# Two graph-attention layers in fp32: the query matrix by halves, the last rows at once, exponentials in even portions

## Chip, cores, metric

One core of a Trainium2 chip. The metric is the device time of one execution in microseconds (us), as the median of several executions; lower is better. Every run quoted gave a correct result. A ratio is the mean time of one kernel's fast runs over the mean of the fast runs of the kernel before in the same rounds, so it is not quite the quotient of the medians that are quoted beside it. A number in brackets after it is the 95% interval.

## The reference

```python
# N = 2708 rows, D = 1024, fp32; adj about 1% ones
h = relu(layernorm(x))                              # layer 0
e = relu((h @ Wf + bf) @ (h @ Wg + bg).T)
x = x + softmax(where(adj > 0, e, -9e15), axis=1) @ (h @ W + bW)
h = relu(layernorm(x))                              # layer 1
hW = h @ W1;  f1, f2 = hW @ a1, hW @ a2
e = leaky_relu(f1 + f2.T, 0.2)
x = x + relu(softmax(where(adj > 0, e, -9e15), axis=1) @ hW)
```

All biases are zero in the data.

## The kernel before

Layer 0 is not computed as written. The kernel forms M = Wf Wg^T once, then q = h M, scores = q h^T plus rank-one terms for the biases, and it projects by W only after the aggregation. The rows fall into five **panels** of queries (586, 586, 512, 512, 512) and eleven **pairs** of row tiles; pair 2 is the **short pair**, two tiles of 74 rows. Each large product is done with seven half-size products M1 to M7 in place of eight (the scheme of Strassen and Winograd), so operands are first added and subtracted on VectorE and stored to device memory (`hs_d` for the scores, `hg_d` for the aggregation, `md_d` for q), then loaded as needed.

Work off TensorE's path is handed out by credit. Each group of matmuls may draw a number of microseconds of background work:

```python
def put(us, go, fetch=None, takes_psum=False):
    later.append([us, fetch, go, takes_psum])

def behind(us, psum_free=False):            # called after a group of matmuls
    credit[0] = min(credit[0] + us, 2 * us)
    while later and credit[0] > 0 and (psum_free or not later[0][3]):
        credit[0] -= one()                  # the first item of `later`, whole
```

An item is drawn whole as soon as any credit is left. The order of instructions on each engine is fixed when the program is built.

A pair is normalized in place (`norms`), its sums for the aggregation are stored (`rows`), its dot products taken (`dots`), it is transposed, and its sums for the scores are stored (`sums`):

```python
EARLY = 6
for q in range(NQ):                         # NQ = 11
    put(4.2, norms(q), fetch(q));  put(2.7, rows(q));  put(3.2, dots(q))
    if q < EARLY:
        put(0.5, transposes(q), takes_psum=True);  put(2.7, last(q))   # last: sums, stores
for q in range(EARLY, NQ):
    put(0.5, transposes(q), takes_psum=True);  put(2.7, last(q))
# ... sums(q): the short pair's stores are cut to n = 74 of 128 columns (296-byte runs)
    nc.gpsimd.dma_start(hs_d[q][:, 0:4, :, :n]..., lo[:, :, :, :n]...)
```

The end of a projection in layer 0 adds the residual and stores it; then the rows of layer 1 are made:

```python
def go(t, e, c):                            # e: left or right half of the row tile t
    add(xs[t][e], c, xs[t][e])
    nc.gpsimd.dma_start(x1_d[t][:n, ...], xs[t][e])
    if seen[t] == 2:
        rows_done(t, xs[t])                 # put(2.1, normalize); put(3.2, dots); ...
```

In layer 1 an item of the exponentials is one row tile of P, handed out at 2.0 while a projection group gave a credit of 6.0.

## Time and profile before

| | before |
|---|---|
| median of three runs | 3357.59 us (3354.02 to 3358.53) |
| span of the profiled execution | 3363.8 us |
| TensorE busy | 94% |
| sum of TensorE's gaps over 0.5 us | 185 us |

TensorE is the bound, so what counts is its gaps and the slow matmuls that follow them (16 passes took 8.53 us after a gap of 10.00, and 7.03 before it). "L414" in a line is line 414 of the kernel; the figure in square brackets is the idle time of the engine before the group and what ended it. The lines that carry this are in the prediction below.

### The profile page before, as it was taken

The page shows a single profiled execution, that of the slowest core. Times are in us where ns is not written, and L with a number is a line of the kernel's source. Part 1 is how long each engine was busy: PE and PEld are TensorE (multiplying, and loading weights), DVE is VectorE, ACT ScalarE, POOL GpSimd, SP SyncE. Part 2 cuts the span into 40 slices and gives each one's busy share as a digit, 9 for nine tenths or more (in the row PEclk, how much of TensorE's full clock was granted, in tenths as well). Part 3 has the DMA queues.
Part 4 walks back from the last instruction along what each step waited for, and adds up shares of the span by engine and source line. Part 5 has one row for each costly group of instructions (what it writes and reads, how often), then busy time and mean ns, then how long its engine had stood idle before and what let it go on. Part 6 is the DMA issues. An engine that isn't in the chain of part 4 may idle for free.

```text
span 3363.8 us, 34967 instructions
## 1 busy us (share of the span) xinstructions
PE 3165.5 (94%) x12924; PEld 2336.2 (69%) x12924; DVE 1733.8 (52%) x3606; ACT 497.5 (15%) x832; POOL 369.9 (11%) x423
## 2 busy tenths in 40 slices
PE   8768999999999989999999999996989999999998
PEld 4346776757877468885888885854757738678584
DVE  5666568165541664616672358449273362734612
ACT  2222020010110100201020002004040120301200
POOL 1421001210002110011000102020010000000001
PEclk9889999999999989999999999997999999999999
DMA  5898658576643576547664466675435355454645
GB/s 206 264 335 278 210 183 313 177 219 194 196 147 132 166 208 215 178 157 236 205 210 158 143 215 214 235 258 198 144 124 201 127 166 189 150 203 153 209 140 197
DMA packets 273714, 660.56 MB, mean 196 GB/s; under 512 B 54604, under 2 KB 124224, under 8 KB 272264
## 3 DMA queue, kind: packets, MB, share of 16 engines
q1 hardware_dynamic: 237080, 543.04, 49.3%
q0 software_dynamic: 36464, 115.29, 9.9%
q8 instruction: 102, 1.67, 0.2%
q14 instruction: 68, 0.56, 0.0%
HBM read 542.97 MB, written 115.13 MB: 196 GB/s over the span
## 4 chain that ended last, share of the span: by engine, by line
PE 40%; issue 6%; DVE 4%; DMA 1%; POOL 1%; ACT 0%; SPq 0%; POOLq 0%; DVEq 0%; ACTq 0%
PE gz L414 10%; PE gy L414 8%; PE gx L414 8%; PE sz L833 3%; PE pz L731 3%; PE sx L833 2%; PE sy L833 2%; PE py L731 1%; DVE P L1014 1%; DVE sm L198 1%; DVE P L198 1%; PE px L731 1%; PE qz L414 1%; PE qy L414 0%; PE qx L414 0%
## 5 line engine op out<-in xcount | busy, mean ns | idle before, releaser
L833 PE MATMUL sz<-B,As 128*128 128x256 f32 (+3 forms) x1320 | 334.0, 396 | 14.7 <-DVE st L198 14.0
L414 PE MATMUL gz<-P,hc 128*128 128x256 f32 (+3 forms) x1320 | 307.6, 392 | 0.0
L833 PEld LDWEIGHTS sz<-B,As 128*128 128x128 f32 (+1 forms) x1320 | 246.4, 188 | 77.3 <-DVE st L198 19.5
L414 PEld LDWEIGHTS gz<-P,hc 128*128 128x128 f32 (+1 forms) x1320 | 248.6, 190 | 48.7
L833 PE MATMUL sx<-B,As 128*128 128x256 f32 (+3 forms) x880 | 229.4, 403 | 15.1 <-DMA As<-hs_d 13.0
L414 PE MATMUL gx<-P,hc 128*128 128x256 f32 (+3 forms) x880 | 211.7, 401 | 11.8 <-ACT P L1016 11.8
L833 PE MATMUL sy<-B,As 128*128 128x256 f32 (+3 forms) x880 | 219.3, 391 | 0.7 <-DMA As<-hs_d 0.7
L414 PE MATMUL gy<-T,hc 128*128 128x256 f32 (+3 forms) x880 | 206.2, 395 | 6.4 <-DMA hc<-hg_d 6.4
L668 POOL TENSOR_TENSOR gT<-gT,rr 128x2048 f32<-128x2048 f32 (+3 forms) x20 | 68.3, 3437 | 1307.3 <-ACT rr L137 742.6
L414 PEld LDWEIGHTS gx<-P,hc 128*128 128x128 f32 (+1 forms) x880 | 169.6, 194 | 54.0 <-ACT P L1016 18.8
L414 PE MATMUL gz<-Sa,hc 128*128 128x256 f32 (+3 forms) x880 | 206.7, 393 | 0.0
L731 PE MATMUL py<-w,ps 128*128 128x512 f32 (+1 forms) x352 | 168.0, 630 | 37.2 <-DVE pt L198 30.7
L833 PEld LDWEIGHTS sx<-B,As 128*128 128x128 f32 (+1 forms) x880 | 163.1, 191 | 51.9 <-DMA As<-hs_d 14.1
L414 PEld LDWEIGHTS gy<-T,hc 128*128 128x128 f32 (+1 forms) x880 | 168.1, 191 | 43.0 <-DMA hc<-hg_d 7.8
L833 PEld LDWEIGHTS sy<-B,As 128*128 128x128 f32 (+1 forms) x880 | 162.9, 185 | 39.0 <-DMA As<-hs_d 1.1
L414 PEld LDWEIGHTS gz<-Sa,hc 128*128 128x128 f32 (+1 forms) x880 | 165.4, 190 | 32.1
L198 DVE TENSOR_TENSOR gT<-gz,m 128x256 f32<-128x256 f32 (+1 forms) x80 | 34.7, 438 | 269.5 <-PE gz L414 269.5
L731 PEld LDWEIGHTS py<-w,ps 128*128 128x128 f32 (+1 forms) x352 | 68.9, 198 | 130.6 <-issue 93.4
L731 PE MATMUL pz<-w,ps 128*128 128x512 f32 (+1 forms) x352 | 155.5, 593 | 0.4 <-DMA w<-wt_d 0.3
L731 PE MATMUL px<-w,gT 128*128 128x512 f32 x320 | 142.2, 595 | 5.4 <-ACT P L1013 3.0
L537 ACT COPY mask<-mk_ps 128x1024 bf16<-128x1024 bf16 (+1 forms) x55 | 55.6, 1010 | 611.2 <-PE mk_ps L536 336.6
L731 PEld LDWEIGHTS pz<-w,ps 128*128 128x128 f32 (+1 forms) x352 | 65.3, 186 | 86.8 <-issue 83.7
(237 smaller groups left out, 4609.0 us busy)
## 6 DMA issues: line engine op xcount, KB each, us to landing
hc<-hg_d SPq DMA_DIRECT2D x280, 704.0 KB
As<-hs_d SPq DMA_DIRECT2D x150, 512.0 KB
w<-wt_d SPq DMA_DIRECT2D x96, 512.0 KB
w<-in_L_gnn_W_dram SPq DMA_DIRECT2D x72, 512.0 KB
md<-md_d SPq DMA_DIRECT2D x70, 512.0 KB
adj_i<-in_adj_dram SPq DMA_DIRECT2D x50, 512.0 KB
hg_d<-g POOLq DMA_DIRECT2D x40, 512.0 KB, 6.1
As<-hs_d SPq DMA_DIRECT2D x50, 256.0 KB
```

Of the source, the lines that this page charges most:

```text
L198: nc.vector.tensor_tensor(o, a, b, OP.add)
L414: nc.tensor.matmul(acc[d][:, :h], ls(k), right(m, k), start=(start and k == 0), stop=(k == K - 1), skip_group_check=True)
L537: nc.scalar.copy(mk[:n, :, :k4 * P], ps[:n, :, :k4 * P])
L668: nc.gpsimd.tensor_tensor(of(e, s), of(e, s), by(s, k), OP.mult)
L731: nc.tensor.matmul(ps, left[i][m][:, k, :], w_[k], start=(start and k == 0), stop=(k == NH - 1), skip_group_check=True)
L833: nc.tensor.matmul(ps[:n, :h], A[i // 2][:, i % 2, c, :n], B[m][c // 2][:, c % 2, :h], start=(start and c == 0), stop=(c == NH - 1), skip_ ...
L1014: nc.vector.scalar_tensor_tensor(s, ub[:n, :w], f[1][:n, t:t + 1], s, op0=OP.add, op1=OP.max)
```

## The change

Its intent: (1) make M in two column halves, so that the first product can begin with half of the right factor, and do four pairs ahead of q in place of six, with the starts of further pairs interleaved with their ends; (2) treat the last panel's rows at once as their projection ends, so that layer 1 can begin sooner; (3) hand out the exponentials of layer 1 evenly; (4) take the residual rows of the last projection from another buffer pool, so that they hold up no weights.

```diff
-    EARLY = 6
+    EARLY, AHEAD = 4, 5
...
+        for q in range(EARLY):
+            start(q)                        # norms, rows, dots
+            end(q)                          # transposes, sums and stores
+        for q in range(EARLY, EARLY + AHEAD):
+            start(q)
         for q in range(EARLY, NQ):
-            put(0.5, lambda q=q: transposes(q), takes_psum=True)
-            put(2.7, lambda q=q: last(q))
+            end(q)
+            if q + AHEAD < NQ:
+                start(q + AHEAD)
...
+    transposed_wg(0)
+    for a in range(NC):
+        half_row_of_M(a, 0)                 # first half of the columns, all eight row blocks
+        if a == NH: ... transposed_wg(1)
+        if a >= NH: behind(6.5, True)
+    for k in range(NH):
+        for a in (k, k + NH):
+            half_row_of_M(a, 1)
+            behind(6.5, True)
+        left_of_q(k)
...                                         # q's products: M1 M5 M2 M6 M3 M7 M4 before
+        accumulate(left, right, NH, h, (M1, M2, M5, M6, M3, M7, M4), then, evict, "q",
...                                         # the aggregation's second operand: after M5, not M1
-                   {M1: second, M2: fourth, ...
+                   {M5: second, M2: fourth, ...
...                                         # rows_done
+        if panel_of[t] == NP - 1:
+            normalize(xt)
+            dots()
+            raise_max(0, q, k, first_mask[t][:n, :width[0]])
+            if whole:
+                ... pair_h(1, q, ...)       # last pair: between the transposes and the reductions of shifts1(0)
+                for p in range(1, NP):
+                    put_max(p, q)
+            return
...                                         # weights1, finish1, end of the program
-            put(2.0, lambda i=i, mk=mk: go(i, mk), ...
+            front.append([2.1, ..., (lambda i=i, mk=mk: go(i, mk)), False])
+        later[:0] = front
...
-                xs[t] = row_halves("x1_res", n, True)
+                xs[t] = row_halves("x1_res", n, p < NP - 1)
...
-        project(1, p, g, finish1(), by_pair=(p == NP - 1), rate=6.0)
+        project(1, p, g, finish1(p), by_pair=(p == NP - 1), rate=1.7)
```

More of the change, by code (lines that the diff above doesn't have):

```diff
@@ L302, in last, with start, end @@
             made[0] = q + 1
-        for q in range(NQ):
-            put(4.2, lambda q=q: norms(q), lambda q=q: fetch(q))
-            put(2.7, lambda q=q: rows(q))
-            put(3.2, lambda q=q: dots(q))
-            if q < EARLY:
-                put(0.5, lambda q=q: transposes(q), takes_psum=True)
-                put(2.7, lambda q=q: last(q))
+        def start(q):
+            put(4.2, lambda: norms(q), lambda: fetch(q))
+            put(2.7, lambda: rows(q))
+            put(3.2, lambda: dots(q))
+        def end(q):
+            put(0.5, lambda: transposes(q), takes_psum=True)
+            put(2.7, lambda: last(q))
+        for q in range(EARLY):
[3 more added lines that the diff above has]
+            start(q)
         for q in range(EARLY, NQ):
-            put(0.5, lambda q=q: transposes(q), takes_psum=True)
-            put(2.7, lambda q=q: last(q))
+            end(q)
+            if q + AHEAD < NQ:
+                start(q + AHEAD)
     def make_until(q):
@@ L323, in load_rows, with transposed_wg @@
         return t
-    bfb = row_to_all(bf, "bfb")
-    wgT = [[slot(f"wgT{c}_{b}") for b in range(2)] for c in range(NC)]
-    for b in range(2):
+    bfb, bgb = row_to_all(bf, "bfb"), row_to_all(bg, "bgb")
+    wgT, wfT, M = [None, None], {}, {}
+    def transposed_wg(b):
         ws = [load_rows(wg, 4 * b + i, "wg") for i in range(4)]
+        wgT[b] = [slot(f"wgT{c}_{b}")[:, :W] for c in range(NC)]
         for c in range(NC):
@@ L332 @@
                 nc.tensor.transpose(ps[:, i * P:(i + 1) * P], ws[i][:, c * P:(c + 1) * P], ident)
-            copy(wgT[c][b][:, :W], ps)
+            copy(wgT[b][c], ps)
         for i in range(4):
             dot(u[:, 4 * b + i:4 * b + i + 1], halves(ws[i]), halves(bfb))
-    bgb = row_to_all(bg, "bgb")
-    wfT = {}
     def transposed_wf(a):
@@ L347, in transposed_wf, with store_M, half_row_of_M, left_of_q @@
         dot(v[:, a:a + 1], halves(wt), halves(bgb))
-    M = {}
-    def row_of_M(a, background):
-        M[a] = []
-        for b in range(2):
-            ps = bank("M_ps")
-            for c in range(NC):
-                nc.tensor.matmul(ps, wfT[a][c // NH][:, c % NH, :], wgT[c][b][:, :W], start=(c == 0), stop=(c == NC - 1))
-            M[a].append(slot(f"M{a}_{b}"))
-            copy(M[a][b][:, :W], ps)
-            if background:
-                behind(6.5, True)
-        wfT.pop(a)
-    def left_of_q(a):
-        k = a % NH
-        store = lambda m, s: nc.gpsimd.dma_start(md_d[:, m, k, :], s)
-        if a < NH:
-            store(M1, M[k][0][:, :W])
-            return
-        a11, a21, a12, a22 = (t[:, :W] for t in M.pop(k) + M.pop(k + NH))
+    def store_M(m, k, s):
+        nc.gpsimd.dma_start(md_d[:, m, k, :], s)
+    def half_row_of_M(a, b):
+        ps = bank("M_ps")
+        for c in range(NC):
+            nc.tensor.matmul(ps, wfT[a][c // NH][:, c % NH, :], wgT[b][c], start=(c == 0), stop=(c == NC - 1))
+        M[a, b] = slot(f"M{a}_{b}")[:, :W]
+        copy(M[a, b], ps)
+        if b == 0:
+            store_M(M1 if a < NH else M2, a % NH, M[a, b])
+    def left_of_q(k):
+        a11, a12, a21, a22 = M.pop((k, 0)), M.pop((k + NH, 0)), M.pop((k, 1)), M.pop((k + NH, 1))
         s1, s2, s4 = (slot(f"ms{i}")[:, :W] for i in range(3))
         add(s1, a21, a22)
-        store(M5, s1)
-        store(M2, a12)
+        store_M(M5, k, s1)
         sub(s2, s1, a11)
-        store(M6, s2)
+        store_M(M6, k, s2)
+        sub(s4, a12, s2)
+        store_M(M3, k, s4)
         sub(a21, a11, a21)
-        sub(s4, a12, s2)
-        store(M3, s4)
-        store(M7, a21)
-        store(M4, a22)
+        store_M(M7, k, a21)
+        store_M(M4, k, a22)
     make_pairs()
-    for i, a in enumerate((0, 4, 1, 5, 2, 6, 3, 7)):
-        if i == 0:
-            transposed_wf(0)
-            transposed_wf(4)
+    transposed_wg(0)
+    ahead = [0, 1, 2, 3, 4, 5, 6, 7]
+    for a in range(NC):
+        for _ in range(2):
+            if ahead:
+                transposed_wf(ahead.pop(0))
+        half_row_of_M(a, 0)
+        if a == NH:
             dot(c0, halves(bfb), halves(bgb))
-        if i == 2:
-            for k in (1, 5, 2, 6, 3, 7):
-                transposed_wf(k)
             vb = [slot(f"vb{g}") for g in range(2)]
@@ L394, with accumulate @@
                 spread(vb[g][:, :W], [v[:, 4 * g + j:4 * g + j + 1] for j in range(4)])
-        row_of_M(a, i >= 2)
-        left_of_q(a)
-    def accumulate(left, right, rows, K, h, then, evict, name, prepare={}, psum_after=(), rate=0.0):
-        X = None
-        for m, start in ((M1, True), (M5, True), (M2, False), (M6, True), (M3, False), (M7, False), (M4, False)):
+            transposed_wg(1)
+        if a >= NH:
+            behind(6.5, True)
+    for k in range(NH):
+        for a in (k, k + NH):
+            half_row_of_M(a, 1)
+            wfT.pop(a)
+            behind(6.5, True)
+        left_of_q(k)
+    def accumulate(left, right, K, h, order, then, evict, name, prepare={}, rate=0.0):
+        for m in order:
+            start = m in (M1, M5, M6)
             if m == M1:
@@ L487, in project_q @@
                  M4: lambda d, ps: plus(part(B[M2], d), ps, ub(d + NH), part(m1, d))}
-        accumulate(left, right, NH, NH, h, then, evict, "q",
+        accumulate(left, right, NH, h, (M1, M2, M5, M6, M3, M7, M4), then, evict, "q",
                    {M1: second, M2: fourth, M3: lambda: sides(M3), M7: lambda: sides(M7), M4: lambda: sides(M4)},
@@ L564, in load_mask, with column_max @@
         return mt
-    def column_max(p, acc):
+    def column_max(p, acc, between=None):
         m = stats.tile([P, 5], FP, name="mcol")
         nc.vector.memset(m, 0.0)
-        o = 0
+        o, turned = 0, []
         for i, (_, n) in enumerate(panels[p]):
@@ L575, in column_max @@
             nc.tensor.transpose(ps[:n, i % 4, :], acc[:, o:o + n], ident)
-            nc.vector.tensor_reduce(m[:n, i:i + 1], ps[:n, i % 4, :], AX.X, OP.max)
+            turned.append(ps[:n, i % 4, :])
             o += n
+        if between:
+            between()
+        for i, (_, n) in enumerate(panels[p]):
+            nc.vector.tensor_reduce(m[:n, i:i + 1], turned[i], AX.X, OP.max)
         return m
@@ L668, in scale @@
                 nc.gpsimd.tensor_tensor(of(e, s), of(e, s), by(s, k), OP.mult)
-        accumulate(left, right, NH, NQ, h, then, evict, "g",
-                   {M1: second, M2: fourth, M3: lambda: inverse.append(column_sum_inverse(p, sm)), M7: scale}, rate=rate)
+        accumulate(left, right, NQ, h, (M1, M5, M2, M6, M3, M7, M4), then, evict, "g",
+                   {M5: second, M2: fourth, M3: lambda: inverse.append(column_sum_inverse(p, sm)), M7: scale}, rate=rate)
         nc.vector.tensor_tensor(of(1, lo), of(1, lo), by(lo, h), OP.mult)
@@ L722, in project @@
             acc, tmp = {}, {}
-            for m, start in ((M1, True), (M2, False), (M5, True), (M6, True), (M3, False), (M7, False), (M4, False)):
+            for m in (M1, M2, M5, M6, M3, M7, M4):
+                start = m in (M1, M5, M6)
                 w_ = ws.pop(m) if m in ws else load_W(l, m)
@@ L893, in softmax, with shifts1 @@
         return sm
-    done_rows = {}
+    def shifts1(p, between=None):
+        k, t0 = len(panels[p]), first[p]
+        top = column_max(p, mx[p], between)[:, :k]
+        f1 = f[0][:, t0:t0 + k]
+        z, m, c = (stats.tile([P, 5], FP, name=nm)[:, :k] for nm in ("z", "m1", "none"))
+        nc.vector.tensor_add(z, f1, top)
+        nc.vector.scalar_tensor_tensor(m, z, ALPHA, z, op0=OP.mult, op1=OP.max)
+        nc.vector.tensor_scalar(c, top, -BIG / 2, None, op0=OP.is_ge)
+        nc.vector.tensor_mul(m, m, c)
+        nc.vector.tensor_scalar(c, top, -BIG / 2, -BIG, op0=OP.is_lt, op1=OP.mult)
+        nc.vector.tensor_add(m, m, c)
+        sub(z, f1, m)
+        nc.vector.scalar_tensor_tensor(m, f1, ALPHA, m, op0=OP.mult, op1=OP.subtract)
+        return z, m
+    done_rows, first_mask = {}, {}
     def rows_done(t, xt):
@@ L905, in dots, with met @@
             nc.vector.tensor_scalar(f2s[:n, t:t + 1], f[1][:n, t:t + 1], ALPHA, None, op0=OP.mult)
+        q, k = pair_of[t]
+        whole = all(s in done_rows for s in pairs[q])
+        if panel_of[t] == NP - 1:
[3 more added lines that the diff above has]
+            if whole:
+                if q == NQ - 1:
+                    got["zm"] = shifts1(0, lambda: pair_h(1, q, *(done_rows[s] for s in pairs[q])))
+                else:
+                    pair_h(1, q, *(done_rows[s] for s in pairs[q]))
+                for p in range(1, NP):
+                    put_max(p, q)
+            return
+        def met():
+            known.add(q)
+            for p in range(NP):
+                if generated[p] > q:
+                    put_max(p, q)
         put(2.1, lambda: normalize(xt))
         put(3.2, dots)
-        q, _ = pair_of[t]
-        if all(s in done_rows for s in pairs[q]):
-            def met():
-                known.add(q)
-                for p in range(NP):
-                    if generated[p] > q:
-                        put_max(p, q)
+        if whole:
             put(2.7, lambda: pair_h(1, q, *(done_rows[s] for s in pairs[q])))
@@ L927, in start @@
                 r0, n = tiles[t]
+                if p == NP - 1:
+                    first_mask[t] = load_mask(0, *pair_of[t])
                 xs[t] = row_halves("x_res", n, t in short)
@@ L976 @@
                                                  M7: lambda p=p: first_masks(p + 1, 2)})
+    flush()
     project(0, NP - 1, G.pop(NP - 1), finish0(NP - 1), by_pair=True)
-    flush()
-    def shifts1(p):
-        k, t0 = len(panels[p]), first[p]
-        top = column_max(p, mx[p])[:, :k]
-        f1 = f[0][:, t0:t0 + k]
-        z, m, c = (stats.tile([P, 5], FP, name=nm)[:, :k] for nm in ("z", "m1", "none"))
-        nc.vector.tensor_add(z, f1, top)
-        nc.vector.scalar_tensor_tensor(m, z, ALPHA, z, op0=OP.mult, op1=OP.max)
-        nc.vector.tensor_scalar(c, top, -BIG / 2, None, op0=OP.is_ge)
-        nc.vector.tensor_mul(m, m, c)
-        nc.vector.tensor_scalar(c, top, -BIG / 2, -BIG, op0=OP.is_lt, op1=OP.mult)
-        nc.vector.tensor_add(m, m, c)
-        sub(z, f1, m)
-        nc.vector.scalar_tensor_tensor(m, f1, ALPHA, m, op0=OP.mult, op1=OP.subtract)
-        return z, m
     def weights1(p, z, m):
@@ L1020, in go, with finish1 @@
             exps[0] += 1
+        front = []
         for i in range(len(order) + LAG):
             mk = []
-            put(2.0, lambda i=i, mk=mk: go(i, mk),
-                (lambda i=i, mk=mk: mk.append(load_mask(p, *order[i]))) if i < len(order) else None)
+            front.append([2.1, (lambda i=i, mk=mk: mk.append(load_mask(p, *order[i]))) if i < len(order) else None,
+                          (lambda i=i, mk=mk: go(i, mk)), False])
+        later[:0] = front
         return S, sm
-    def finish1():
+    def finish1(p):
         xs = {}
@@ L1046, in take_shifts @@
     def take_shifts(p):
+        flush()
         got["zm"] = shifts1(p)
@@ L1050, in take_weights @@
         got["P"] = weights1(p, *got["zm"])
-    take_shifts(0)
     take_weights(0)
```

## The prediction

> **What bounds the kernel now.** I read the page first (busy shares), then the waits, then TensorE's own timeline for the whole span, and last the busy time of each engine in chosen stretches.
>
> ```profile
> PE 3165.5 (94%) x12924; PEld 2336.2 (69%) x12924; DVE 1733.8 (52%) x3606; ACT 497.5 (15%) x832; POOL 369.9 (11%) x423
> ```
>
> TensorE is the bound: 94% of the span. So the change can only earn what TensorE now loses: its gaps, and the slow matmuls after a gap. Adding up every gap over 0.5 us in TensorE's timeline gives 185 us. They sit in four places: the start (65 us before the scores of panel 0), the scores of panels 2 and 3 (28 us), the end of layer 0 with the first exponentials of layer 1 (about 38 us) and the projections of layer 1 (40 us). The diff goes at the first, third and fourth.
>
> The start, by stretch (columns: stretch, length, busy time and count of PE, PE weight loads, DVE, ACT, POOL, then granted clock, DMA share, GB/s):
>
> ```profile
> 60.00:70.00 10.00, 10.00 (x51) 6.41 (x50) 5.25 (x9) 4.37 (x7) 1.62 (x3) 1.00 0.41 150
> ...
> 130.00:140.00 10.00, 10.00 (x24) 4.37 (x23) 0.00 (x0) 0.00 (x0) 3.14 (x4) 1.00 0.83 183
> 140.00:150.00 10.00, 0.60 (x2) 0.00 (x0) 0.55 (x1) 2.15 (x4) 2.29 (x4) 0.70 0.71 233
> ...
> 180.00:190.00 10.00, 0.00 (x0) 0.00 (x0) 9.21 (x24) 3.13 (x6) 4.32 (x9) 0.58 0.99 354
> 190.00:200.00 10.00, 0.00 (x0) 0.00 (x0) 1.48 (x5) 0.28 (x1) 1.36 (x2) 0.50 1.02 298
> ```
>
> Two idle stretches of TensorE, each with a falling clock. TensorE's timeline names what ended the second:
>
> ```profile
> 204.99 10.06 PE L414 MATMUL qx<-hT,md 128*128 128x293 f32 x32 [25.96 <-DMA md<-md_d]
> ```
>
> The product M (16 half rows at 6.95 us) ends at 179, but q's first matmul waits until 205. The load queue issues the hT tiles only at 187.6: hT shares its buffer with hsT, so it waits for the last of the six early pairs to be written out. The wait of 18.2 us at 140.6 is for x of the fifth pair, behind a VectorE that stood still from 124.3 to 149.5.
>
> A projection of layer 1 (panel 0), TensorE:
>
> ```profile
> 2473.87 7.03 PE L731 MATMUL px<-w,gT 128*128 128x512 f32 x16
> 2482.62 7.11 PE L731 MATMUL px<-w,gT 128*128 128x512 f32 x16 [1.72 <-ACT pt L737]
> ...
> 2513.46 8.53 PE L731 MATMUL py<-w,ps 128*128 128x512 f32 x16 [10.00 <-DVE pt L198]
> ```
>
> and engine busy time for it, and for the end of layer 0:
>
> ```profile
> 2216.00:2302.00 86.00, 54.66 (x127) 23.92 (x125) 63.87 (x141) 13.68 (x21) 18.74 (x22) 0.82 0.87 301
> ...
> 2474.00:2536.00 62.00, 50.28 (x115) 21.93 (x114) 49.40 (x74) 23.08 (x36) 3.86 (x7) 0.92 0.54 175
> ```
>
> In the projection VectorE is full for the first 39 us, with exponentials handed out three at a time, and part idle for the last 20: TensorE waits for an addition queued behind them.
>
> [...] clock 0.50 to 0.58 in the idle stretches above, and the 16 passes after the 10 us gap take 8.53 us, not 7.03. So a removed long gap is worth about 1.5 us more than its length. [...] the trace has 0.69 us for 128x512, so VectorE's work can simply be counted. [...] The trace has the short pair (rows of 296 B) landing in about 22 us where a full pair takes 6.5, and 298 to 354 GB/s at most over the saturated stretches. [...]
>
> **Part 1: M by halves, four pairs ahead.** (a) First M product: 28.9 us now, after all 4 MB of the right factor. Then 2 MB of it, one row block of the left and the two bias rows (about 3.5 MB at 330 GB/s, after a start of 7 us) give some 20. But the second half's transposes (4.5 us of TensorE) come later, in the middle, so by the point where the background work starts TensorE is only some 5 us ahead. (b) Four whole pairs instead of six: the last early pair is the fourth, so hT comes free some 25 to 30 us before M is done and not after it. Two pairs' transposes (3.7 us each) leave this stretch, and with no fifth pair's transposes queued before M's next half rows the wait of 18.2 us goes. VectorE will still stand some 20 us behind the short pair's write, but TensorE then has the half rows left and banks for them. (c) q's order M1, M2, M5 lets two products run on the two operands stored first.
> M then ends near 155 to 160; hT is loaded by about 165 to 172 with a busy DMA. Before, two of q's seven products were done at 225.5; after: 168+16 = 184, though M5 needs a VectorE operand, due near 180 to 190. That is a gain of about 40. The five products left take 8 us each, as now: 224 to 230. I allow 7 to 10 for loads that come late from a busy DMA, so the scores start at 231 to 240 instead of 272, **36 us** earlier. Check by bytes: 51 MB were moved by 205; two pairs' hs tiles and half a pair's rows less make 47.6. At 60 us about 13 are done; the other 34.6 at 290 GB/s take 119, so 179. q's operands are not last in line, so 168 to 175 is still possible, but DMA is now the floor.
> (d) Given back: seven pairs end inside the scores of panel 0 instead of five (+7.4 us of TensorE, but that is what left M's stretch and is counted there), and two starts. As per query pair needs 1.84 MB, masks 0.9, an end 2.1: up to 340 GB/s for the first nine query pairs, at the limit. In return the burst of four pairs' transposes at 286 (waits 4.8 and 0.7) is gone. I take 7.4 more TensorE time, 6 less waiting, and 5 of DMA waits: 6 back. **Net 30 us** (18 to 42).
>
> **Part 2: last rows of layer 0.** From TensorE's last projection matmul (2275.0) to the spread of the shifts (2295.4) are 20.4 us. After: two additions 1.8, statistics and their ACT step 2.9, dots 3.3, one maximum 0.8, transposes hidden under the pair's sums 2.7, five reductions 1.2, eight small operations 1.3: 14 us. Gained: 6. The reductions no longer alternate with the transposes, and eight of the 0.74 us maxima move behind the aggregation. Within the projection (59.3 us for 48.1 of passes) the treatment at once puts the first group's rows ahead of the second group's sums on VectorE; the wait of 5.95 may shrink or move. I take 3. **9 us** (2 to 14). The slow first product (about 14 us lost, 2.1 us an exponential, VectorE-bound) stays.
>
> **Part 3: exponentials of layer 1.** A product of two groups is 16 passes, 6.87 us; seven make 48.1 (21 groups of panel 1: 72.1). Measured from first matmul to the aggregation's first: 61.7, 81.2, 60.4, 59.7. Lost: 13.6, 9.1, 12.3, 11.6 = 46.6. After, at 1.7 us of credit and 2.1 an item, 11 exponentials fall into the 14 steps (10 having gone into the last aggregation product); the last three go behind the next aggregation, which may take them because its second step now comes after M5, not M1. VectorE then has 11 x 2.13 + 17.8 of sums and additions + 1.4 = 42.6 us in 48: tight but even. The wait for ACT's first copy (1.4 to 1.7) stays, and I allow one more per projection: 10 in all. **36 us** (28 to 41).
>
> **Part 4: the last projection.** Its residual rows move from the stream buffers to slots, so the weights' load is not held up: the wait of 6.02 on w at 3325, and the slow matmuls after it (about 1.5). **7 us.**
>
> Sum: 30 + 9 + 36 + 7 = 82; 3357.6 - 82 = **3276 us**.
>
> **Rivals.** (R1) DMA takes over at the start: the two idle stretches shrink but the waits reappear as As or md loads in q and the scores of panel 0. For: DMA share 0.94 to 1.02 from 180 to 272. Against: 0.59 to 0.61 from 360 to 420, so there is room to move into. Part 1 would then be worth 12 and the time 3294. (R2) VectorE becomes the projection's bound: 42.6 of 48 us leaves little for an order fixed in advance; half of part 3 stays lost: 3294. (R3) Treating the rows at once starves the second group: its sums wait for two tiles' norms and dots (about 13 us of TensorE), and part 2 is worth -3: 3288. (R4) Better than thought: M5 not held, no DMA waits: part 1 gives 45, time 3260.
>
> **Range and chances.** Parts 3 and 4 are the surest, part 1 the widest. Spreads of 10, 5, 5 and 2 us, and some for reordering elsewhere, give about 20: range 3250 to 3306. The 2% line is 3357.6 x 0.98 = 3290.4, some 14 us above the centre: faster 0.75, within 2% 0.24, slower 0.01.
>
> **What would show it.** First M matmul near 20; q's first matmul at 165 to 175 and the first score near 235; scores of panel 0 still about 178 long; about 14 us from the last projection matmul of layer 0 to the spread; projections of layer 1 at 50 to 52 us with no wait over 3 us on pt; no wait on w in the last. I am wrong if waits of several us on As or hT turn up in the first 400 us, or if pt waits stay.

## The result, and the profile after

| | before | after |
|---|---|---|
| median | 3358.06 us (3354.02 to 3361.71, 4 runs) | 3341.61 us (3336.16 to 3345.40, 4 runs) |
| ratio | | 0.995 [0.9932, 0.9968] |
| profiled span, granted clock | 3363.8 us, 0.971 | 3343.4 us, 0.973 |
| TensorE: first M matmul | 28.9 | 24.9 |
| last M matmul ends | 177.3 | 152.6 |
| first q matmul | 205.0 | 191.0 |
| first score | 272.0 | 254.4 |
| scores of panel 0 end | 449.9 | 452.4 |
| first projection of layer 0 starts | 672.0 | 680.8 |
| last projection of layer 0 | 2215.7 to 2275.0 | 2224.5 to 2296.2 |
| first aggregation matmul of layer 1 | 2302.4 | 2324.4 |
| last matmul | 3355.2 | 3334.8 |

The kernel is half a per cent faster, not the 2.4% predicted. The marks say where: layer 1 takes 1010.4 us in place of 1052.8, a gain of 42.4, and 22.0 of it had been lost by its beginning. The start, which was to gain 30, loses 8.8 by the first projection. From there to the last projection of layer 0 nothing changes (1543.7 us in both). That projection and the passage to layer 1 take 99.9 us in place of 86.7, a loss of 13.2.

**The start.** TensorE's timeline of the kernel after:

```profile
24.89 7.03 PE L364 MATMUL M_ps<-wgT,wfT 128*128 128x512 f32 x16
...
144.75 7.89 PE L364 MATMUL M_ps<-wgT,wfT 128*128 128x512 f32 x18
190.96 4.45 PE L422 MATMUL qx<-hT,md 128*128 128x293 f32 x9 [38.31 <-DMA md<-md_d]
...
284.94 4.28 PE L846 MATMUL sz<-B,As 128*128 128x293 f32 x8 [8.29 <-DVE st L198]
```

M is done 25 us earlier, and then TensorE waits 38 us, not 26, for q's operands. And the scores of panel 0 have two new waits of over 8 us (the other stands at 304.1), both for an addition on VectorE. DMA in two stretches of the kernel after (columns as in the prediction; the last two are DMA share and GB/s):

```profile
110.00:140.00 30.00, 29.96 (x82) 14.02 (x81) 13.47 (x35) 5.20 (x11) 11.70 (x13) 1.00 0.63 137
...
180.00:190.00 10.00, 0.00 (x0) 0.00 (x0) 0.74 (x2) 0.00 (x0) 1.04 (x2) 0.50 0.99 327
```

From 110 to 140 the DMA engines move 137 GB/s at 0.63 of their time; afterwards they are full until q can begin (350 GB/s at 1.02 from 140 to 191). ScalarE's timeline and then VectorE's show what stood still meanwhile:

```profile
141.48 0.58 ACT L272 COPY hsT<-h_ps 128x512 f32<-128x512 f32 x1 [16.55 <-DMA hs_d<-hsT]
```

```profile
127.69 0.21 DVE L176 SCALAR_TENSOR_TENSOR r<-part,c 128x1 f32<-128x1 f32 x1
144.38 0.69 DVE L201 TENSOR_TENSOR hsT<-hsT,a 128x512 f32<-128x512 f32 x1 [16.48 <-ACT a L272]
```

The fourth pair cannot be copied into hsT, which has one buffer, until the short pair has been stored out of it. VectorE waits for ScalarE, and what the two would have made is not stored. This pause is not the whole of the hole: GpSimd goes on issuing what is ready, and the rate is lowest before the pause (79 GB/s from 110 to 120, 213 from 130 to 140, inside it). The load queue waits too, 12.0 us from 107 to 119, for a store of rows (`hg_d<-x`). And q's left operands hT are loaded into the buffer that hsT leaves, so their first load is issued only 5.4 us after M's end. The load queue (SyncE) in the kernel after:

```profile
158.07 2.22 SPq L98 DMA_DIRECT2D hT<-hs_d  x2
```

The DMA issues of the kernel after, from 100 to 160 us (transfer, queue, count, KB each, us to landing), show the short pair (592 KB) against a whole pair (1024 KB), then the same for sums of the aggregation:

```profile
hs_d<-hsT POOLq DMA_DIRECT2D x2, 1024.0 KB, 10.1
...
hg_d<-g POOLq DMA_DIRECT2D x2, 512.0 KB, 8.5
hg_d<-g POOLq DMA_DIRECT2D x2, 296.0 KB, 21.0
hs_d<-hsT POOLq DMA_DIRECT2D x1, 592.0 KB, 21.7
```

**The scores of panel 0.** VectorE's timeline ahead of the wait at 276.6:

```profile
273.54 0.69 DVE L212 BATCH_NORM_STATS2 bn<-x 128x6 f32<-128x512 f32 x1
...
283.36 0.21 DVE L176 SCALAR_TENSOR_TENSOR r<-part,c 128x1 f32<-128x1 f32 x1
283.49 0.82 DVE L198 TENSOR_TENSOR sm<-sx,rb 128x293 f32<-128x293 f32 x2
```

A whole start of a pair (10 us, 273.5 to 283.4), behind the end of another (from 271.6), stands ahead of the addition `sm` that frees TensorE's banks.

**The end of layer 0.** TensorE's timeline of the kernel after (before: waits of 5.95 and 2.00 us in the projection, and 13.70 ahead of the transposes `mx_ps`):

```profile
2262.27 5.95 PE L744 MATMUL px<-w,gT 128*128 128x512 f32 x8 [9.06 <-issue]
2275.04 6.41 PE L744 MATMUL py<-w,ps 128*128 128x512 f32 x8 [6.81 <-DVE ps L198]
...
2313.32 1.33 PE L583 MATMUL mx_ps<-ident,mx 128*128 128x128 f32 x5 [17.09 <-DVE mx L807]
```

The first ends with ScalarE's copy at 2261.61. ScalarE's timeline:

```profile
2250.70 0.81 ACT L220 ACTIVATE x_res<-x_res,rs 128x512 f32<-128x512 f32 x1 [4.66 <-DMA x_d<-x_res]
...
2260.19 1.52 ACT L220 ACTIVATE x_res<-x_res,rs 128x512 f32<-128x512 f32 x2 [1.96 <-DMA x_d<-x_res]
2261.61 0.56 ACT L750 COPY pt<-px 128x512 f32<-128x512 f32 x1
```

The rows are normalized in place, in the tile that has just been handed to a store, so each activation waits until that store has read it, and the copy that TensorE needs stands behind in ScalarE's order. In the second wait VectorE shows one maximum of 6 us beside nine others of 0.70 to 0.82. VectorE, then GpSimd at the same time:

```profile
2267.03 6.03 DVE L807 SCALAR_TENSOR_TENSOR mx<-maskl,f,mx 128x586 f32<-128x586 bf16 x1
```

```profile
2267.51 4.91 POOL L976 TENSOR_TENSOR x_res<-x_res,bwb 128x512 f32<-128x512 f32 x4
```

**Layer 1.** The projection of panel 0, to compare with the lines in the prediction:

```profile
2496.66 7.03 PE L744 MATMUL px<-w,gT 128*128 128x512 f32 x16
2505.42 7.11 PE L744 MATMUL px<-w,gT 128*128 128x512 f32 x16 [1.72 <-ACT P L1042]
...
2526.09 7.03 PE L744 MATMUL py<-w,ps 128*128 128x512 f32 x16
...
2547.73 12.51 PE L422 MATMUL gx<-P,hc 128*128 128x293 f32 x50
```

The wait of 10 us is gone: 51.1 us from the first matmul to the aggregation's first, in place of 61.7. The last projection, before and then after:

```profile
3331.11 3.75 PE L731 MATMUL py<-w,ps 128*128 128x512 f32 x4 [6.02 <-DMA w<-wt_d]
```

```profile
3312.88 3.67 PE L744 MATMUL px<-w,gT 128*128 128x512 f32 x8 [0.72 <-issue]
```

No wait for w is left there (the projection of panel 1 has three new ones, 2.8 us together). Parts 3 and 4 do what was predicted; parts 1 and 2 are the question.

### The profile page after: what moved, and what is told of

The parts are those of the page before. It is cut to its first block, busy times and chain, and to the rows that moved or that the text cites. A ratio compares the mean times of both kernels' runs of the same rounds, so it can differ in the third digit from the quotient of the medians.

```text
span 3343.4 us, 34899 instructions
## 1 busy us (share of the span) xinstructions
PE 3159.0 (94%) x12924; PEld 2337.7 (70%) x12924; DVE 1743.4 (52%) x3606; ACT 498.9 (15%) x832; POOL 369.0 (11%) x423
## 4 chain that ended last, share of the span: by engine, by line
PE 43%; issue 4%; DVE 3%; DMA 1%; ACT 0%; POOL 0%; POOLq 0%; DVEq 0%; SPq 0%; ACTq 0%
PE gz L422 12%; PE gy L422 8%; PE gx L422 8%; PE sz L846 3%; PE pz L744 3%; PE sx L846 2%; PE sy L846 2%; PE px L744 2%; PE py L744 1%; DVE sm L198 1%; PE qz L422 1%; DMA w<-wt_d 0%; DVE P L1043 0%; PE qx L422 0%; PE qy L422 0%
## 5 line engine op out<-in xcount | busy, mean ns | idle before, releaser
L422 PEld LDWEIGHTS gy<-T,hc 128*128 128x128 f32 (+1 forms) x880 | 168.4, 191 | 40.2 <-DVE Sa L201 4.8
L744 PE MATMUL py<-w,ps 128*128 128x512 f32 (+1 forms) x352 | 158.7, 602 | 9.4 <-DVE ps L198 6.8
```

The costliest lines, as they stand in the source:

```text
L422: nc.tensor.matmul(acc[d][:, :h], ls(k), right(m, k), start=(start and k == 0), stop=(k == K - 1), skip_group_check=True)
L744: nc.tensor.matmul(ps, left[i][m][:, k, :], w_[k], start=(start and k == 0), stop=(k == NH - 1), skip_group_check=True)
```

## The experiments

All kernels had three rounds beside the kernel before, whose medians were 3361.59 (e1 to e4), 3362.96 (e5 to e8), 3360.91 (e9 to e12) and 3363.78 us (e13 to e15).

### e1: the change without part 1

```diff
-    EARLY, AHEAD = 4, 5
+    EARLY = 6        # and M, the order of pairs and q's order as in the kernel before
```

> The changed kernel with its first part undone: M in whole rows, six pairs ahead, q's products in the old order; the rest stays. Theory: the first part wins 17.6 us up to the first scores (254.4 against 272.0) and gives them back, 20 us in the scores of panel 0 (198 against 178) and some 6 us in the first aggregation, so it is worth about -9 us; then this kernel takes 3332 us, ratio to the kernel before 0.9925. Rival (the prediction's): the first part is a gain that something else hides; then this kernel is slower than the changed one, 3350 us or more.

Measured: 3334.38 us, 0.9921 [0.9905, 0.9938]; the first score at 272.4. Without part 1 the change is faster than with it, by 0.0029 or about 10 us. The two ran in different rounds and their intervals just touch, so the profiles have to carry it, and they agree: the first projection of layer 0 starts at 670.9 in e1 and at 680.8 with the change.

### e2: the change without part 2

```diff
-        if panel_of[t] == NP - 1:
-            normalize(xt) ... return        # all rows put behind, as before
-    flush()
     project(0, NP - 1, G.pop(NP - 1), finish0(NP - 1), by_pair=True)
+    flush()
...
+    take_shifts(0)
```

> The changed kernel with the treatment of the last rows of layer 0 undone. Theory: the treatment at once lengthens the last projection of layer 0 from 59 to 72 us and does not shorten what follows it (28.2 us against 27.4 to the first aggregation of layer 1), so undoing it gives 13 us: 3328 us, ratio 0.991. Rival: that projection is longer for another reason (what the first part left behind, or the queue of loads); then still 3341 us.

Measured: 3326.03 us, 0.9901 [0.9884, 0.9918]. Part 2 costs about 16 us. From the last projection's first matmul to the first of layer 1 it is 85.9 us here, against 99.9 with the change.

### e4: the kernel before with parts 3 and 4 alone

```diff
         # in the kernel before
-            put(2.0, ... go(i, mk) ...)
+            front.append([2.1, ..., go(i, mk), False])      # and later[:0] = front
-        project(1, p, g, finish1(), by_pair=(p == NP - 1), rate=6.0)
+        project(1, p, g, finish1(p), by_pair=(p == NP - 1), rate=1.7)
```

> The kernel before with only the exponentials of layer 1 handed out evenly, the second step of the aggregations after M5, and the last residual rows in slots. Theory: the parts add up, and this one is worth 42 us by the profiles (layer 1 from its first aggregation matmul to its last projection matmul: 1052.8 before, 1010.4 after): 3316 us, ratio 0.9875. Rival: part of the 42 us was lent by the other parts; then 3325 us or more.

Measured: 3320.92 us, 0.9882 [0.9867, 0.9896], 40 us. The two parts need nothing of the rest. With e1 and e2 the sum closes roughly: a gain of 40, less 10 and 16, leaves 14, where the change itself gives 17 (0.995).

### e3: part 2 with the normalized rows in tiles of their own

```diff
-            normalize(xt)
+            x1, xt = xt, row_halves("h1", n)
+            done_rows[t] = xt
+            normalize(x1, xt)
```

> The changed kernel, but the last panel's rows are normalized into tiles of their own and not in place: same instructions. Theory: the in-place activation has to wait until the store of the same tile has been read (4.7, 2.0, 2.3 and 4.1 us on ScalarE), which also keeps ScalarE from copying the next group's first product, so TensorE waits 9.05 us. With tiles of their own the 9.05 us go and 4 us of the tail after the last matmul: 3328 to 3332 us. Rival: the wait is VectorE's, for a mask whose load stands behind a weight load (6.8 us on TensorE); then at most 1 or 2 us change.

Measured: 3333.71 us, 0.9919 [0.9904, 0.9933]. TensorE's timeline of the last projection:

```profile
2248.59 5.33 PE L746 MATMUL px<-w,gT 128*128 128x512 f32 x8 [2.77 <-issue]
2264.08 6.13 PE L746 MATMUL py<-w,ps 128*128 128x512 f32 x8 [10.15 <-DVE ps L198]
```

The first wait falls from 9.06 to 2.77 us, so it was the store of the same tile. The second grows from 6.81 to 10.15: VectorE does its eight maxima before the sums all the same. From the projection's first matmul to the first of layer 1 it is 92.3 us (99.9 with the change, 86.7 before).

### e5: and the maxima of the other panels after the last pair

```diff
         # e3, and
-                for p in range(1, NP):
-                    put_max(p, q)
+                if q == NQ - 1:
+                    for q in range(NQ - 2, NQ):
+                        for p in range(1, NP):
+                            put_max(p, q)
```

> As e3 (last rows normalized into tiles of their own), and the maxima of panels 1 to 4 over the last two pairs are put behind only after the very last pair. Theory: with the stores out of the way, what still delays the second group's sums are eight maxima ahead of them on VectorE, which took 10.8 us in e3 because one waits for a mask whose load stands behind a weight load; TensorE waited 10.15 us. Without them there the last projection of layer 0 falls from 68 to about 58 us: 3323 us, ratio 0.989 (e3 had 0.9919). Rival: VectorE simply has too much to do in that stretch, whatever the order; then the wait moves and the ratio stays at 0.991 or more.

Measured: 3329.25 us, 0.9892 [0.9867, 0.9916], 86.9 us for the passage. The wait ahead of py is 5.39. It did not go with the maxima: the operation that now stood at that place, the first of the pair sums, took 5.95 us itself. I had put the maximum of 6 us down to a mask loaded late; a pair sum reads no mask. That was taken up in e13.

### e6: the short pair as a whole pair, padded with zeros on GpSimd

```diff
+                full = row_halves("x", P)
+                    nc.gpsimd.memset(full[e], 0.0)          # for the short tiles
-                    load(xs[q][-1][e], x[r0:r0 + n, ...])
+                    load(full[e][:n], x[r0:r0 + n, ...])
...
-            n = rows_of[q]                  # in transposes, sums and pair_h of layer 0
+            n = P
```

> The changed kernel with the short pair (74 rows each) padded by rows of zeros to 128, so that its h, sums and transposes are stored like those of a full pair and not in runs of 296 bytes from 74 rows. Theory: q's first product waits at 153 to 191 because DMA loses some 30 us of its rate between 110 and 140 (79 to 213 GB/s) behind that pair's stores; then DMA is full to 210. With whole stores (about 1.6 MB more to move, 5 us) the first q product comes 12 to 20 us earlier, near 175, and the scores near 238: about 3328 us, ratio 0.991. Rival: DMA is bound by its bytes alone from 80 on; then q starts at 191 or later and the time is 3341 us or more.

Measured: 3345.30 us, 0.9943 [0.9918, 0.9967]. A flawed test. The load queue of the kernel e6 waited for the memset:

```profile
SPq L98 <- POOL x L255: 51.4, 2, 50.9
```

M ended at 168.4 in place of 152.6, and q began at 191.2. It tells nothing of the short pair; e9 repeats it without the memset.

### e7: seven starts ahead

```diff
-    EARLY, AHEAD = 4, 5
+    EARLY, AHEAD = 4, 7
```

> The changed kernel with all seven other pairs started before the first of them is ended (seven ahead, not five), so that no norms and dots are left for the scores of panel 0. Theory: the two waits of 8.3 and 8.6 us there come from a start of 10 us and an end standing together on VectorE ahead of the next query pair's additions; without starts there the scores of panel 0 take about 180 us, not 198. The starts go into q's products, where DMA is full (2.85 MB each), so q gets longer by 4 to 12 us: 3327 to 3335 us, ratio 0.991. Rival: it is DMA that makes those scores long; then they stay near 195 us.

Measured: 3338.76 us, 0.9923 [0.9899, 0.9948]. The scores of panel 0 take 184.4 us in place of 198.0, and the waits of 8.29 and 8.63 us are gone: they were the starts in the middle of the scores. Part of it returns, for the ends now come four at once (a wait of 3.91 in the middle of their transposes), and q waits 4.41 for a right operand.

### e8: halves, but six pairs ahead

```diff
-    EARLY, AHEAD = 4, 5
+    EARLY, AHEAD = 6, 5
```

> The changed kernel with M by halves but six pairs ended ahead of q, as in the kernel before (and five started after). It splits the first part: the order of M alone. Theory: making M by halves is worth only its earlier start (some 8 us), the wait of 18 us for the fifth pair's rows comes back, q starts near 198 and the scores of panel 0 take 178 us again; so 3325 to 3335 us, ratio 0.991. Rival: the fewer pairs are what gains at the start and the halves do nothing; then q starts at 205 and the time is near that of e1, 3334 us.

Measured: 3341.27 us, 0.9929 [0.99, 0.9958]. M ends at 170.2 and q begins at 204.9, as before the change, after a wait of 32.9. Halves by themselves bring q no nearer; it takes fewer pairs as well. Fewer pairs with whole rows of M were not run.

### e9: the short pair filled with the rows that follow it

```diff
-                xs[q].append(row_halves("x", n))
+                full = row_halves("x", P)
+                xs[q].append(full)
-                    load(xs[q][-1][e], x[r0:r0 + n, ...])
+                    load(full[e], x[r0:r0 + P, ...])        # 54 rows that nobody reads later
...
-            n = rows_of[q]                  # in transposes, sums and pair_h of layer 0
+            n = P
```

> e6 once more without its flaw: there the rows of zeros were written by GpSimd behind its stores, and the load queue stood 51 us for that. Here the short pair is filled up with the rows that follow it in x (real numbers, never used), so no instruction is added. Theory, as in e6: the hole in DMA's rate between 110 and 140 goes, q's first product comes 12 to 20 us before 191, the scores near 238; the scores of panel 0 stay 198 us long: about 3327 us, ratio 0.991. Rival: DMA is bound by its bytes from 80 on, then q starts at 188 or later and the ratio is 0.994 or more.

Measured: 3327.87 us, 0.9902 [0.9887, 0.9917]. The same two stretches in e9, then its TensorE:

```profile
110.00:140.00 30.00, 30.00 (x83) 14.17 (x83) 27.19 (x63) 11.61 (x21) 13.69 (x22) 1.00 1.02 368
...
180.00:190.00 10.00, 7.02 (x29) 4.80 (x27) 7.24 (x21) 4.55 (x9) 1.93 (x3) 1.00 1.03 364
```

```profile
175.28 10.50 PE L423 MATMUL qx<-hT,md 128*128 128x293 f32 x32 [22.76 <-DMA md<-md_d]
```

The load queue of e9:

```profile
141.28 2.33 SPq L98 DMA_DIRECT2D hT<-hs_d  x2
```

368 GB/s in place of 137, with more bytes to store; VectorE is busy for 27 of 30 us, not 13; the first hT is issued 16.8 us earlier, before M's end; q begins 15.7 us earlier and the first score comes at 239.3 in place of 254.4. So the hole behind the short pair's stores was what kept q late. The scores themselves are as long as before the repair (195.6 us, the same two waits).

### e10: the old order of q's products

```diff
-        accumulate(left, right, NH, h, (M1, M2, M5, M6, M3, M7, M4), then, evict, "q",
+        accumulate(left, right, NH, h, (M1, M5, M2, M6, M3, M7, M4), then, evict, "q",
```

> The changed kernel with q's products in the old order (M1, M5, M2, ...). Theory: the new order is what costs some 5 us in the first aggregation (a wait of 6.5 us on hc at 525, with one hc tile loaded ahead and not three); with the old order those come back: 3336 us, ratio 0.9935. At the start it loses little, as q waits for DMA either way. Rival: the wait on hc comes from the pairs' later ends; then it stays, and the ratio is 0.995.

Measured: 3338.34 us, 0.9932 [0.9913, 0.9952]. The wait of 6.52 us on hc in the first aggregation (TensorE at 531.80 after the change) is gone, but q itself then waits 4.87 and 2.81, and two smaller waits on hc come up, 3.98 and 3.71: the first aggregation takes 168.2 us, where it took 172.0 with the change and 165.4 before. The interval overlaps that of the change, so a gain of this edit alone is not shown.

### e11: the start spread out, without part 2

```diff
         # e2, and
-    EARLY, AHEAD = 4, 5
+    EARLY, AHEAD = 4, 7
-        (M1, M2, M5, M6, M3, M7, M4)       # q
+        (M1, M5, M2, M6, M3, M7, M4)
-            behind(6.0, True)              # in scores, after each pair
+            behind(6.0 if p else 3.2, True)
```

> The candidate: last rows of layer 0 as before, q's products in the old order, four pairs ended and all others started ahead of q, and in the scores of panel 0 one pair ended per query pair (credit 3.2 and not 6.0). Theory: without bursts on VectorE or ScalarE the scores of panel 0 take about 178 us from about 262, so they end at 440 and not 450; with the 40 us of layer 1: 3311 us, ratio 0.985 (e4 had 0.9882). Rival: DMA sets that stretch whatever the order; then it ends at 448 or later and the ratio is 0.988.

Measured: 3307.96 us, 0.9844 [0.9828, 0.986]. With a credit of one end for each pair of queries, the scores of panel 0 take 173.2 us (177.9 before, 198.0 with the change) and their longest wait is 2.76. Against e2 this is a gain of about 19 us. From e7 to e11 the number of ends in the scores stays the same and the scores are 11.2 us shorter, so that much was the lumps of background work and not its amount. The 13.6 us of e7 are lumps and amount together, since two starts left the scores there.

### e12: and the short pair whole

The edits of e11 and e9 together.

> e11 with the short pair stored whole, as in e9. Theory: the two gains add, as q then starts some 15 us earlier: 3299 us, ratio 0.981. Rival: once the starts fill q's stretch, the DMA time gained at the start is only spent later: ratio 0.985 as in e11.

Measured: 3292.03 us, 0.9798 [0.9783, 0.9812]. q begins at 174.7, the first score comes at 247.0, the scores end at 420.3 (449.9 before). It beats both kernels.

### e13: the change without the additions of the bias in the last panel

The bias is zero here, so the result stays right; it is a test, not a version.

```diff
-                    nc.gpsimd.tensor_add(xs[t][e], xs[t][e], bwb[e][:n, :W])
+                    if p < NP - 1:
+                        nc.gpsimd.tensor_add(xs[t][e], xs[t][e], bwb[e][:n, :W])
```

> The changed kernel without the four GpSimd additions of the bias to the residual rows of the last panel in layer 0 (the bias is zero in this case's data, so the result stays right). Theory L (GpSimd's additions hold VectorE): the maximum of 6.03 us at 2267 falls to about 0.75, the wait of 6.81 us before the second group's py to about 1.5, the wait of 9.06 before px stays, and the time falls by 5 to 6 us, ratio about 0.9935. Rival K (the mask of that maximum arrives late): the 6 us stay, and the time too, ratio 0.995.

Measured: 3334.16 us, 0.9906 [0.9883, 0.993]. The maxima of e13 in the last projection, with their shortest, median and longest duration in ns, then TensorE:

```profile
L807 DVE SCALAR_TENSOR_TENSOR mx<-maskl,f,mx x10: 696/746/825, 2254.4 to 2271.8; 128x512 f32<-128x512 bf16 x6, 128x586 f32<-128x586 bf16 x4
```

```profile
2262.48 5.71 PE L744 MATMUL px<-w,gT 128*128 128x512 f32 x8 [9.35 <-issue]
2270.05 3.70 PE L744 MATMUL py<-w,ps 128*128 128x512 f32 x8 [1.86 <-DVE ps L198]
```

No maximum takes 6 us any more, the wait falls from 6.81 to 1.86 us, and the one ahead of px stays. GpSimd's additions held VectorE; the late mask falls. The passage takes 89.5 us in place of 99.9, more than the 5 expected: the slower matmuls after the gap (6.41 us to 3.70) and 2.8 us of the wait ahead of the maxima's transposes (14.29 in place of 17.09) went too.

### e14: part 2 repaired

```diff
         # e5, and
-                    nc.gpsimd.tensor_add(xs[t][e], xs[t][e], bwb[e][:n, :W])
+                    (nc.gpsimd if p < NP - 1 else nc.vector).tensor_add(...)
```

> e5 with the bias of the last panel added on VectorE (four operations of 0.69 us, 2.8 us) in place of GpSimd. L: the first pair sum of the second group takes 0.7 us in place of 5.95, py waits some 2.5 us less than the 5.39 of e5, and from the projection's first matmul to layer 1's first gx are about 84.5 us (86.9 in e5, 86.7 in the kernel before). Ratio about 0.9885 against 0.9892 of e5. Rival K: 5.95 stays, and the four additions come on top: 89.5 us, ratio 0.990.

Measured: 3328.68 us, 0.9887 [0.9865, 0.9909]. The pair sum takes 0.69 us in place of 5.95. Yet the passage takes 85.9 us, 1.0 less than in e5 and not 2.4: TensorE has one wait of 8.79 us in place of two that made 8.16. With the hold gone, VectorE's own work is what fills that place: additions, statistics, dots and the sums behind them.

### e15: the best version with part 2 repaired

The edits of e11 to the start and to the scores, with those of e9 and e14.

> e12 (the best so far, 0.9798, without part 2) with part 2 put back in the form of e14. L: 2 to 3 us better than e12, about 0.979, with about 84.5 us from the projection's first matmul to the first gx. If the part is worth nothing even so, 0.980 to 0.981.

Measured: 3296.01 us, 0.9787 [0.9762, 0.9811], against e12's 0.9798 [0.9783, 0.9812]: no difference is shown. The passage takes 86.2 us, 88.1 in e12. On the way there e15 waits 20.7 us for As in the scores of panels 1 to 4, e12 13.4; why, I have not traced.

## Why the prediction was wrong

**What held.** TensorE was the bound and the gain came from its gaps. Part 3 was put at 36 us: four projections now lose 10.5 us in place of 46.6, so 36. Part 4 was put at 7: the last projection takes 50.6 us in place of 58.1, so 7.5. M's end "near 155 to 160" came at 152.6, and VectorE stood 16.5 us behind the short pair where some 20 were foreseen.

Two readings in the prediction were off without harm: 179 is the end of the transposes behind M, whose last matmul ended at 177.3; and "298 to 354 GB/s at most" holds for the stretches listed there only (the kernel before moved 406 GB/s from 100 to 110 us).

**Step (a).** The first M matmul was to come at some 20 us and came at 24.9. Little hung on it: in e8 M ends 7 us earlier than before (170.2 for 177.3) and q begins where it did (204.9 for 205.0).

**Steps (b) and (c), the first that failed.** Step (b) let hT's buffer come free 25 to 30 us before M is done, and (c) had "hT is loaded by about 165 to 172 with a busy DMA". But the first hT was issued at 158.1, 5.4 us after M's end, and q began at 191. The pause behind the short pair was seen, but counted for TensorE only ("TensorE then has the half rows left and banks for them"). The same slow store keeps hsT from the fourth pair, so the fourth pair is stored late, hsT is given up late, and hT is loaded late, with all else that was put off: from the first hT to q it takes 33 us, where it took 17 before, with the DMA engines full (342 GB/s at 1.03 from 158 to 191). The prediction's own check by bytes came to 179, and I set it aside. It had the bytes nearly right (about 47.6 MB by 191, worked out from 249 GB/s over the 191 us) and the rate wrong: it took 290 GB/s from 60 us on, an estimate of its own, and it was 254 from 60 to 191; the kernel before had 258 from 60 to 205. With the hole filled (e9), hT is issued at 141.3 and q begins at 175.3, inside the predicted 165 to 175 but for 0.3 us. From hT to q it is then 34 us, as long as with the change, so the earlier hT accounts for the earlier q; what of this is order and what is bytes, e9 does not separate. So the mechanism, fewer pairs and an earlier q, was right, and a cost that the kernel had before the change as well was not carried along. It is true that the diff does not change the short pair's transfers; but a cost that is not changed still comes due when the work around it moves.

**Step (d), the second.** "7.4 more TensorE time, 6 less waiting, and 5 of DMA waits: 6 back" became 20: the scores of panel 0 take 198.0 us in place of 177.9. I counted the items' amount, not where they land. An item is drawn whole, a start costs VectorE 10 us, and one query pair takes 14 us of TensorE; so a start and an end together are longer than the banks can bridge (waits of 8.29 and 8.63 us). e7 (starts moved ahead, two of them out of the scores) takes 13.6 us of it back, and e11 (one end for each query pair as well) 11.2 more, to 173.2. The further 6 us lost by the first projection lie in the first aggregation, which finds one tile of hc loaded where there were three; e10 removes that wait, has two smaller ones in its place, and does not show a gain.

Together, part 1 cost about 10 us (e1) where 30 were to be won. R1 had the place, DMA at the start, but expected it from more load, not from a pause; none of the rivals had the lumps in the scores.

**Part 2.** "9 us" became a loss of 13 in the trace and 16 in e2. Two terms failed. The tail from the last projection matmul to the spread of the shifts was to take 14 us; it took 21.2, against 20.4 before, because each normalization waits for the store of its own tile (2.3 and 4.1 us there), and because nine maxima of some 0.74 us stand in it, of which only two are for panel 0, with which layer 1 begins. And the term "I take 3" for the projection was a loss of 12.5 (71.8 us in place of 59.3). R3 had guarded against starved sums, with a loss of 3. The causes it lacked are separate, and each was removed by itself: the store of the same tile ahead of the copy (e3: 9.06 to 2.77), and the four additions on GpSimd that now fall together beside one maximum of VectorE (e13: the wait ahead of py from 6.81 to 1.86). Before, the same four additions fell among VectorE's operations of all kinds, and the longest operation beside them took 2.03 us.

The traces show the hold elsewhere too: in the kernels before and after, every VectorE operation of over 2 us, nine in each, overlaps a GpSimd addition or scaling (`x_res<-x_res,bwb` or `gT<-gT,rr`), and e13 shows it by taking four of these away (6.03 us becomes at most 0.83). How the hold begins the trace does not settle: the maximum is recorded from 2267.03, the first addition from 2267.51. The prediction counted VectorE's operations at 0.69 us each. In the kernel before that count already failed beside GpSimd, with eight operations of 2.66 to 3.61 us in layer 1 and one of 2.03 at the end of layer 0.

Even repaired, treating the rows at once gains 0 to 2 us in the passage over putting them behind (85.9 in e14 against 85.9 in e2, 86.2 in e15 against 88.1 in e12), within the noise of the whole. The expected 9 us are not there, since VectorE's work fills the stretch in either order.

**Still open.** Why the short pair's stores are slow. Those to `hs_d` have 128 partitions and runs of 296 bytes; those to `hg_d` have 74 rows and runs of 512 bytes, as a whole pair has. The latter were slow too: 296 KB issued at 110.2 us landed 20.5 us later, and the rate was down to 45 GB/s from 115.5 to 118.4, before the first store with 296-byte runs was issued at 119.0. So short runs alone are not the cause; how the cost divides is not known, since e9 changed both. And why the scores of the later panels wait 7 us longer in e15 than in e12.

## What to carry to other kernels

When an idle stretch is to be removed, ask what the idle engine was hiding: here a slow store that paused two engines and the transfers, and whose lost transfers came due when all the rest was early. Background work handed out by credit must come in pieces shorter than the slack of the engine that it stands before; the sum of its cost says little (from e7 to e11 as many ends stand in the scores of panel 0, and these fall from 184.4 to 173.2 us). Before work is done "at once", look at what its operands still owe to others (a store from the same tile, which held ScalarE for 2.0 to 4.7 us here, or work on another engine that slows it, as GpSimd's four additions made a maximum of VectorE 6.03 us in place of some 0.8), for what stood far apart before may now meet.

## What else the traces show of the hardware

- A store of 592 KB from 296-byte runs landed after 21.7 us and one of 1024 KB from whole rows after 10.1, so a quarter of the rate by these two numbers (27 and 101 KB per us). But a store of 296 KB from 74 rows with 512-byte runs took 21.0 where one of 512 KB from whole tiles took 8.5 (14 and 60 KB per us). What the 74 rows, the short runs and the transfers queued beside them cost each, the runs do not separate.
- VectorE was held across a row of four GpSimd instructions (4.91 us; the maximum took 6.03), not for one. In layer 1, beside GpSimd's scaling, each of eight operations took about 3 us (2.66 to 3.62), where the others of their line took 0.73 to 0.83.
- Such a hold does not look like a wait: the operation is recorded as 6.03 us of busy time, with no idle time before it and no releaser. Only its length against the others of its kind (0.70 to 0.83 us) gives it away.
- An activation in place on a tile with a store under way waited for it: 4.7, 2.0, 2.3 and 4.1 us of ScalarE here, with everything behind it in its order. With tiles of their own (e3) TensorE's wait ahead of px fell from 9.06 to 2.77.
